# A two-layer metaformer on one core: pieces of a step's preparation at other units, the image read in front of the weights, column copies on VectorE alone, an image's first inputs through GpSimd's queue

## The chip, the cores and the metric

The kernel runs on one core of one Trainium2 chip. The metric is the device time of one execution in microseconds (us). The engines are TensorE (PE; its weight loads are listed as PEld), VectorE (DVE), ScalarE (ACT), GpSimd (POOL) and SyncE (SP), which here only issues DMAs. Each engine works through its own instructions in the order in which they were put in its queue, and waits on semaphores for the others.

## The reference, cut to what matters

Two images of 96 channels and 128 x 128 pixels, float32, pass two layers. Layer 0 normalizes over the channels, runs four Mamba scans (along rows and along columns, each forwards and backwards), fuses their outputs, adds them to x, and then applies a feed-forward block with values rounded to an 8-bit float. Layer 1 does the same with a 3 x 3 convolution in place of the scans. The change touches layer 0's normalization and scans alone, of which this is the core for one direction:

```
xz = x @ in_w.T                      # 96 -> 2 * 192
xc, z = split(xz)
xc = silu(conv4(xc) + conv_b)        # four taps along the sequence
xdbl = xc @ xproj_w.T                # -> dt_raw (6), B (16), C (16)
dt = softplus(dt_raw @ dt_w.T + dt_b)
for t:                               # 16384 positions, 192 channels, 16 states
    h = exp(dt_t * A) * h + dt_t * B_t * u_t
    y = sum over the states of h * C_t
y = (y + D * xc) * silu(z)
out = y @ outp_w.T                   # 192 -> 96
```

## The kernel before, in words

For each image there are three stages: `normalize` (layer 0's normalization), `mamba` (the scan stage), and `ffn_and_conv` (all the rest). The image lives in SBUF as `acc`, 96 channels by 16384 positions.

**Constants.** Ahead of the first image, SP reads 13 weight tensors, and ScalarE, VectorE and TensorE derive `amat`, `dmat`, `inx` and `gmat` from them. Only after these does `normalize` issue the eight reads of image 0.

**normalize.** 32 tiles of 512 positions each run through a generator `layernorm`: TensorE centers, ScalarE squares, TensorE takes the mean, ScalarE does log and exp, VectorE multiplies. `together` advances the generators in turn, one tile a turn behind the other. The result `xn` is written to DRAM row by row (`xnr`), then transposed by eight strided copies of 2048 positions, of which VectorE and ScalarE take one half each, and written column by column (`xnc`).

**mamba.** Directions are taken in two pairs (rows and columns together; first forwards, then backwards), and a pair is cut into 32 steps of 512 positions: 64 steps an image. The 2 x 192 channels of a pair fill three groups `g` of 128 partitions. A step holds 24 *units*: for each group, eight pairs of states. Unit k of the loop over `k` does, on each engine in this order:

- at even k, SP fetches rows of B for units k + 6 and k + 7 (`fetch`, line 336's `row_tile`), broadcast from DRAM to 128 partitions, and GpSimd multiplies the rows of B for units k + 2 and k + 3 with dt * u (`feed`, which calls `b_part`: lines 345 and 347; line 347 adds the state that enters the step);
- `issue(k, 0)`: the pieces that were put at place 0 of this unit;
- VectorE scans the first state (line 357), then does the product of the unit before with C (line 445), on GpSimd instead for units 2 and 10 of a step (`by_pool`, line 364); ScalarE copies the last column of that unit to `hst` (line 446); TensorE sums the products over the states into PSUM (`sums`, line 361); where a group begins, VectorE multiplies the finished sum with silu(z) (`gated`, line 368);
- ScalarE computes the decays exp(dt * A) of unit k + 2 (line 353, two activations);
- VectorE scans the second state;
- at even k, SP fetches rows of C for units k + 4 and k + 5;
- `issue(k, 1)`: the pieces that were put at place 1 of this unit.

Beside this runs the *prologue* of the next step, cut into pieces, and each piece has a unit and a place in a list written out by hand (`at`). With m counted from 24 units ahead of the step's own unit 0:

- `load`: SP reads the two inputs `xa` (from `xnr`) and `xb` (from `xnc`).
- `conv` for group 1, 0, 2: TensorE's in-projection with the four taps folded in, into the PSUM tile `misc`, of which there is one; `conv_out` (ScalarE) takes it from there. Group 1 holds channels of both directions, and goes through the tile `mix` and two DMAs (`mix`) to interleave them. `silu` (ScalarE) loads another function table, works on all three groups, and loads the first table back.
- `rows`, `rows_out`, `rows_to_dram`: dt_raw, B and C rows by TensorE, copied by ScalarE, written to DRAM by SP for the broadcast reads.
- for each group the *dt chain*: `dt_in` (TensorE), `dt_exp` and `dt_ln` (three ScalarE activations each), `dt_q`, `dt_log`, `dt_sum`, `dt_u` (one GpSimd operation each, lines 295, 298, 301, 305). Its temporaries `e`, `q`, `ln` have one buffer each.
- `gate`, `gate_out`: the z half of the in-projection; `silu` on it.
- `entry` (ScalarE, line 310) and `entering` (GpSimd, line 313): the state that enters the step.

After a group pair is finished, `project` (TensorE) and `collect` (ScalarE) add its output to `acc`.

All order is the program's own: inside these stages a manual schedule keeps each engine's instructions in the order in which the code issues them. Within one unit and place, pieces keep the order of the list, which puts the pieces that empty `misc` first.

The list stands in `prologue`, the loop at the end of `mamba`:

Of the kernel before, what the change touches and what calls it, by code (L numbers as in the profile page):

```python
# [10 lines left out]
F32 = mybir.dt.float32  # L11
# [30 lines left out]
def tile_metaformer(ctx: ExitStack, tc: tile.TileContext, a: dict, out: bass.AP):  # L42
# [19 lines left out]
    ident = const("ident", (128, 128))  # L62
    center = cpool.tile([C, C], F32, name="center")
# [14 lines left out]
    with tc.tile_pool(name="prep", bufs=1) as pp, tc.tile_pool(name="prep_ps", bufs=2, space=PSUM) as pps:  # L78
        alog = pp.tile([128, 2, NG, S], F32, name="alog")
        nc.sync.dma_start(alog, a["alog"])  # L80
        nc.scalar.activation(alog, alog, AF.Exp)
        nc.vector.tensor_scalar_mul(amat, alog, -1.0)

        dskip = pp.tile([128, 2, NG], F32, name="dskip")
        nc.sync.dma_start(dskip, a["dskip"])
        for pi in range(2):
            for g in range(NG):
                nc.vector.tensor_scalar_mul(dmat[:, pi, g, :], ident, dskip[:, pi, g : g + 1])

        inxw = pp.tile([C, 4, DI], F32, name="inxw")  # L90
        nc.sync.dma_start(inxw, a["inx"])
        taps = pp.tile([C, 4, 4, DI], F32, name="taps")
        nc.sync.dma_start(taps, a["taps"].broadcast_to((C, 4, 4, DI)))
        for d in range(4):
            nc.vector.tensor_tensor(inx[:, d], taps[:, d], inxw[:, d, None, :].broadcast_to((C, 4, DI)), ALU.mult)
        outx = pp.tile([C, 2, NG + 1, 128], F32, name="outx")
        nc.sync.dma_start(outx, a["outx"])
        fusew = pp.tile([C, 4, C], F32, name="fusew")
        nc.sync.dma_start(fusew, a["fusew"])
        for pi, pair in enumerate(PAIRS):  # L100

            for g in range(NG + 1):
                ps = pps.tile([128, C], F32, name="ps")
                nc.tensor.matmul(ps, outx[:, pi, g, :], fusew[:, pair[g // 2], :], start=True, stop=True)
                nc.vector.tensor_copy(gmat[:, pi, g, :], ps)
# [37 lines left out]
    blk = 4 * T  # L143

    def read(b, acc, j):

        nc.sync.dma_start(acc[:, bass.ts(j, blk)], a["x"][b, :, bass.ts(j, blk)])

    def normalize(b, acc, xnr, xnc):

        with ExitStack() as st:
            pool = lambda n, bufs, **kw: st.enter_context(tc.tile_pool(name=n, bufs=bufs, **kw))
            full, wp, psp = pool("n1", 1), pool("n2", 3), pool("n_ps", 3, space=PSUM)
            in_order(st)
            nc.scalar.preload_act_table_set("natural_log_exp_and_others")
            xn = full.tile([C, L], F32, name="xn")
            for j in range(L // blk if b == 0 else 1):
                read(b, acc, j if b == 0 else L // blk - 1)

            def one(r):  # L160
                sl = bass.ts(r, T)
                yield from layernorm(acc[:, sl], eps_c[0:C, 0:1], xn[:, sl], wp, psp, 5)
                if (r + 1) % 4 == 0:
                    sl = bass.ts(r // 4, blk)
                    nc.sync.dma_start(xnr[:, sl], xn[:, sl])

            together(*((r, one(r)) for r in range(NT)))
            cols = xn.rearrange("c (h w) -> c w h", w=W)
            for j in range(L // blk):
                stg = wp.tile([C, blk], F32, name="stg")  # L170
                half = blk // W // 2
                for i, eng in enumerate((nc.vector.tensor_copy, nc.scalar.copy)):
                    eng(
                        stg[:, i * half * W : (i + 1) * half * W].rearrange("c (w h) -> c w h", h=W),
                        cols[:, j * 2 * half + i * half : j * 2 * half + (i + 1) * half, :],
                    )
                nc.sync.dma_start(xnc[:, bass.ts(j, blk)], stg)

    def mamba(acc, xnr, xnc):

        with ExitStack() as st:
            pool = lambda n, bufs, **kw: st.enter_context(tc.tile_pool(name=n, bufs=bufs, **kw))
            io, one, two, gen = pool("io", 2), pool("one", 1), pool("two", 2), pool("gen", 4)
# [23 lines left out]
            def prologue(pi, i, d):  # L207
# [5 lines left out]
                def load():  # L213
                    for n, dram in (("xa", xnr), ("xb", xnc)):
                        t = io.tile([C, T + 3], F32, name=n)
                        if i == 0:
                            nc.gpsimd.memset(t[:, T : T + 3] if rev else t[:, 0:3], 0.0)
                            nc.sync.dma_start(t[:, 0:T] if rev else t[:, 3 : T + 3], dram[:, lo : lo + T])
                        else:
                            nc.sync.dma_start(t, dram[:, lo : lo + T + 3] if rev else dram[:, lo - 3 : lo + T])  # L220
# [20 lines left out]
                def mixed(name):  # L241
                    d["mix", name] = one.tile([128, T], F32, name="mix")
                    return d["mix", name]
# [74 lines left out]
                at = [(-2, 1, load), (2, 1, partial(mix, "xc")), (6, 1, partial(silu, "xc"))]  # L318
                at += [(13, 1, partial(mix, "sz")), (28 if first else 22, 1, partial(silu, "sz"))]
                at += [(9, 0, rows), (10, 0, rows_out), (10, 1, rows_to_dram)]  # L320
                for g, k in ((1, 1), (0, 3), (2, 5)):
                    at += [(k, 0, partial(conv, g)), (k + 1, 0, partial(conv_out, g))]
                for g, k in ((1, 12), (0, 17), (2, 20)):
                    at += [(k, 0, partial(gate, g)), (k + 1, 0, partial(gate_out, g))]
                dts = ((24, 25, 26, 27), (31, 32, 33, 34)) if first else ((14, 15, 16, 18), (19, 20, 21, 23))
                for g, ks in enumerate(((10, 11, 12, 14), *dts)):
                    at += [(k, 0, partial(f, g)) for k, f in zip(ks, (dt_in, dt_exp, dt_ln, dt_q))]
                    at += [(ks[3] + m, 0, partial(f, g)) for m, f in ((1, dt_log), (1, dt_sum), (2, dt_u))]
                    if i > 0:
                        at += [((17, 23, 27)[g], 0, partial(entry, g)), (20 + 8 * g, 1, partial(entering, g))]  # L330

                outs = (conv_out, gate_out, rows_out, dt_exp)
                return sorted(at, key=lambda p: (p[0], p[1], getattr(p[2], "func", p[2]) not in outs))
# [60 lines left out]
            def later(k, where, f, *args):  # L394
                todo.setdefault((k, where), []).append(partial(f, *args))

            def issue(k, where):
                for f in todo.pop((k, where), ()):
                    f()

            for k, where, f in prologue(*steps[0], state[0]):
                if k < nu:
                    f()
                else:
                    later(k - nu, where, f)

            def prepare(n):
                if n < len(steps):
                    for m, where, f in prologue(*steps[n], state[n]):
# [3 lines left out]
                        else:  # L413
                            later(k, where, f)
# [24 lines left out]
            def behind(k):  # L439
# [16 lines left out]
                if (g, s) in BY_POOL:  # L456
                    later(k + 1, 1, by_pool, h, c)
                    later(k + 3, 1, sums, s, y, c)
# [4 lines left out]
                if s == S - 2 and g > 0:  # L463
                    later(k + 3, 0, project, pi, i, d, g)
                    later(k + 3, 1, collect, pi, d, g)
# [7 lines left out]
            for k in range(total + 6):  # L473
                n, u = divmod(k, nu)
                if u == nu - 2:
# [120 lines left out]
    acc = accp.tile([C, L], F32, name="acc")  # L596
# [77 lines left out]
```

## Time and profile before

| | |
|---|---|
| median of 3 runs | 12153.81 us (12136.48 to 12159.19) |
| the profiled execution's own time | 12198.56 us |
| its span | 12196.8 us |
| VectorE busy | 10962.5 us, 90% |
| TensorE busy | 10601.0 us, 87% |
| GpSimd busy | 9908.7 us, 81% |
| ScalarE busy | 8585.5 us, 70% |
| first scan of image 0, of image 1 | at 151.4 us, at 6234.8 us |
| last scan of image 0, of image 1 | ends at 5532.9 us, at 11618.2 us |
| last layernorm product of image 0, of image 1 | ends at 81.1 us, at 6166.7 us |
| bytes moved by DMA | 3417 MB, 280 GB/s in the mean |

How to read the lines that follow: a line of a timeline gives the start in us from the start of the span, the duration in us, the engine, the line of the kernel, the operation, the tile written and the tiles read, the shapes, the count, and in brackets the idle time of the engine just before and what ended it. A group's line gives count, busy time, mean duration in ns, and the idle time before its instructions. Idle time of an engine counts only where that engine, or one that waits for it, is the one that sets the end.

### The profile page before, as it was taken

The page shows a single profiled execution, that of the slowest core. Times are in us where ns is not written, and L with a number is a line of the kernel's source. Part 1 is how long each engine was busy: PE and PEld are TensorE (multiplying, and loading weights), DVE is VectorE, ACT ScalarE, POOL GpSimd, SP SyncE. Part 2 cuts the span into 40 slices and gives each one's busy share as a digit, 9 for nine tenths or more (in the row PEclk, how much of TensorE's full clock was granted, in tenths as well). Part 3 has the DMA queues.
Part 4 walks back from the last instruction along what each step waited for, and adds up shares of the span by engine and source line. Part 5 has one row for each costly group of instructions (what it writes and reads, how often), then busy time and mean ns, then how long its engine had stood idle before and what let it go on. Part 6 is the DMA issues. An engine that isn't in the chain of part 4 may idle for free. (4 is left out here: it accounts for less than half of the span.)

```text
span 12196.8 us, 95712 instructions
## 1 busy us (share of the span) xinstructions
PE 10601.0 (87%) x24208; PEld 4012.8 (33%) x24208; DVE 10962.5 (90%) x10624; ACT 8585.5 (70%) x15110; POOL 9908.7 (81%) x5336
## 2 busy tenths in 40 slices
PE   7888888888888888888978888888888888888889
PEld 2333333333333333333323333333333333333333
DVE  6999999999999999995469999999999999999954
ACT  6777777777777777775577777777777777777655
POOL 5998999999998989891159989999989999988811
PEclk9999999999999999999989999999999999999999
DMA  7887888788877878781068888888878878878700
GB/s 250 309 319 302 307 319 313 309 318 312 318 310 306 319 305 310 308 317 47 26 242 307 308 317 312 314 318 313 313 307 308 321 308 316 314 305 309 304 32 13
DMA packets 539169, 3417.07 MB, mean 280 GB/s; under 512 B 67276, under 2 KB 68396, under 8 KB 140696
## 3 DMA queue, kind: packets, MB, share of 16 engines
q1 hardware_dynamic: 538616, 3410.94, 72.9%
q8 instruction: 195, 3.19, 0.1%
q14 instruction: 358, 2.93, 0.1%
HBM read 3289.04 MB, written 54.53 MB: 274 GB/s over the span
## 5 line engine op out<-in xcount | busy, mean ns | idle before, releaser
L345 POOL TENSOR_TENSOR row<-dtu,row 128x2048 f32<-128x2048 f32 x1536 | 6949.9, 4525 | 820.8 <-DMA row<-bcd 658.5
L357 DVE TENSOR_TENSOR_SCAN da<-da,row 128x512 f32<-128x512 f32 x5632 | 6650.2, 1215 | 509.8 <-ACT da L353 187.3
L361 PE MATMUL y<-row,ident 128*128 128x512 f32 x12288 | 5957.9, 618 | 1130.5 <-DVE row L445 1125.7
L353 ACT ACTIVATE da<-dt,amat 128x512 f32<-128x512 f32 x6144 | 4250.4, 692 | 278.7 <-DVE row L357 92.0
L361 PEld LDWEIGHTS y<-row,ident 128*128 128x128 f32 x12288 | 2268.5, 194 | 4643.0 <-issue 2296.4
L445 DVE TENSOR_TENSOR row<-da,row 128x1024 f32<-128x1024 f32 x2816 | 3395.8, 1206 | 1.0 <-DMA row<-bcd 0.9
L446 ACT COPY hst<-da 128x2 f32<-128x2 f32 x2816 | 434.7, 154 | 1423.8 <-DVE row L445 1412.4
L204 PE MATMUL misc<-xa,inx 96*64 96x512 f32 (+1 forms) x2048 | 963.6, 614 | 131.3 <-DMA xa<-xnr 108.0
L204 PE MATMUL misc<-xb,inx 96*64 96x512 f32 (+1 forms) x2048 | 962.3, 613 | 1.9 <-ACT xc L231 1.6
L568 POOL TENSOR_TENSOR acc<-acc,y 96x512 f32<-96x512 f32 x128 | 147.4, 1152 | 987.1 <-DVE y L567 987.1
L357 DVE TENSOR_TENSOR_SCAN row<-da,row 128x512 f32<-128x512 f32 x512 | 616.9, 1205 | 0.0
L364 POOL TENSOR_TENSOR row<-row,row 128x1024 f32<-128x1024 f32 x256 | 602.8, 2355 | 7.1 <-DVE row L357 6.1
L580 PE MATMUL pc<-pad,kw 96*96 96x512 f32 x1152 | 566.7, 593 | 0.0
L452 PE MATMUL y<-xc,dmat 128*128 128x512 f32 x768 | 428.9, 640 | 145.2 <-DVE sz L368 145.2
L295 POOL TENSOR_TENSOR q<-e,q 128x512 f32<-128x512 f32 x384 | 487.5, 1270 | 71.5 <-ACT q L292 71.5
L204 PEld LDWEIGHTS misc<-xa,inx 96*64 96x64 f32 (+1 forms) x2048 | 329.7, 166 | 650.6 <-issue 444.9
L231 ACT ACTIVATE xc<-misc,convb 128x512 f32<-128x512 f32 x256 | 175.8, 687 | 519.7 <-PE misc L204 519.7
L301 POOL TENSOR_TENSOR dt<-dt,ln 128x512 f32<-128x512 f32 x384 | 487.1, 1269 | 30.1
L298 POOL TENSOR_TENSOR ln<-ln,q 128x512 f32<-128x512 f32 x384 | 487.2, 1269 | 20.1
L305 POOL TENSOR_TENSOR dtu<-dt,xc 128x512 f32<-128x512 f32 x384 | 487.1, 1269 | 10.2
L378 PE MATMUL misc<-sz,gmat 128*96 128x512 f32 x1024 | 483.6, 594 | 0.0
L124 DVE TENSOR_TENSOR xq<-xm,rs 96x512 fp8e5<-96x512 f32 x128 | 87.9, 687 | 388.0 <-ACT rs L120 387.9
(81 smaller groups left out, 9340.4 us busy)
## 6 DMA issues: line engine op xcount, KB each, us to landing
row<-bcd SPq DMA_DIRECT2D x3072, 1024.0 KB, 7.1
xc<-mix SPq DMA_DIRECT2D x256, 128.0 KB, 5.3
sz<-mix SPq DMA_DIRECT2D x256, 128.0 KB, 5.4
xa<-xnr SPq DMA_DIRECT2D x124, 193.1 KB, 5.2
xb<-xnc SPq DMA_DIRECT2D x124, 193.1 KB, 5.5
bcd<-rows SPq DMA_DIRECT2D x128, 128.0 KB, 6.7
acc<-in_x_dram SPq DMA_DIRECT2D x16, 768.0 KB, 8.6
xnr<-xn SPq DMA_DIRECT2D x16, 768.0 KB, 4.3
```

Of the source, the lines that this page charges most:

```text
L204: nc.tensor.matmul(ps[rows, :], w(PAIRS[pi][d], k, lo, hi), src[d][:, k : k + T], **se)
L295: nc.gpsimd.tensor_tensor(d["q"], d["e"], d["q"], ALU.subtract)
L298: nc.gpsimd.tensor_tensor(d["ln"], d["ln"], d["q"], ALU.add)
L301: nc.gpsimd.tensor_tensor(d["dt"][g], d["dt"][g], d["ln"], ALU.add)
L305: nc.gpsimd.tensor_tensor(dtu, d["dt"][g], d["xc"][:, g, :], ALU.mult)
L345: nc.gpsimd.tensor_tensor(b, d["dtu"][g][:, None, :].broadcast_to((128, 4, T)), b, ALU.mult)
L353: nc.scalar.activation(da[:, j, :], d["dt"][g], AF.Exp, scale=amat[:, pi, g, s + j : s + j + 1])
L357: nc.vector.tensor_tensor_scan(h[:, j, :], da[:, j, :], b[:, j, :], 0.0, ALU.mult, ALU.add)
L361: nc.tensor.matmul(y, ident, c[:, j, :], start=False, stop=s + j == S - 1)
L364: nc.gpsimd.tensor_tensor(c, h, c, ALU.mult)
L445: nc.vector.tensor_tensor(c, h, c, ALU.mult)
L580: nc.tensor.matmul(pc, kw[:, t, :], rows, start=t == 0, stop=t == 8)
```

## The change

**The prologue's pieces stand at other units.** `load` moves from -2 to -3; conv of groups 1, 0, 2 from units 1, 3, 5 to 1, 5, 9, and `conv_out` from place 0 to place 1 of the unit after; `silu` of xc from 6 to 11; `rows` from 9 to 13 and its two followers with it; `gate` from 12, 17, 20 to 11, 18, 21; the dt chains of the three groups, which began at 10, 14 and 19, begin at 15, 17 and 22, and their `dt_q` stands at place 1 of units 17, 22 and 26; `silu` of sz from 22 (28 in the first step) to 31, that is unit 7 of the step itself; `entry` and `entering` move a few units back; `project` and `collect` one unit later. Pieces of different steps that meet at one unit and place are now ordered together, those that empty `misc` first; `rank` carries that.

**The image is read in front of the weights.** `acc` and the reads of image 0 stand right after `ident`; what derives weights becomes a generator `prep` that runs among the layernorm tiles from turn 8 on, and its own reads are issued there.

**Column copies.** 16 copies of 1024 positions, all on VectorE, from a pool of three buffers that is opened after the layernorm tiles.

**First inputs.** For an image's first step in the forward pair, `xa` and `xb` are read through GpSimd's queue. Pools of `mamba` are opened in another order, and `mix` has a pool of its own.

```diff
     ident = const("ident", (128, 128))
+    acc = accp.tile([C, L], F32, name="acc")
+    blk = 4 * T
+
+    def read(b, acc, j):
+
+        nc.sync.dma_start(acc[:, bass.ts(j, blk)], a["x"][b, :, bass.ts(j, blk)])
+
+    for j in range(L // blk):
+        read(0, acc, j)
...
+        alog, dskip = load("alog", (128, 2, NG, S)), load("dskip", (128, 2, NG))
+        outx, fusew = load("outx", (C, 2, NG + 1, 128)), load("fusew", (C, 4, C))
+        inxw, taps = load("inx", (C, 4, DI)), load("taps", (C, 4, 4, DI), spread=True)
+        yield
...
-            full, wp, psp = pool("n1", 1), pool("n2", 3), pool("n_ps", 3, space=PSUM)
+            wp, psp = pool("n2", 3), pool("n_ps", 2, space=PSUM)
...
-            together(*((r, one(r)) for r in range(NT)))
+            streams = [(r, one(r)) for r in range(NT)]
+            with ExitStack() as weights:
+                together(*streams, *([(8, prep(weights))] if b == 0 else []))
+            stg = pool("n3", 3)
             cols = xn.rearrange("c (h w) -> c w h", w=W)
-            for j in range(L // blk):
-                stg = wp.tile([C, blk], F32, name="stg")
-                half = blk // W // 2
-                for i, eng in enumerate((nc.vector.tensor_copy, nc.scalar.copy)):
...
+            part = 8
+            for j in range(W // part):
+                t = stg.tile([C, part, W], F32, name="stg")
+                nc.vector.tensor_copy(t, cols[:, bass.ts(j, part), :])
+                nc.sync.dma_start(xnc[:, bass.ts(j, part * W)], t.rearrange("c w h -> c (w h)"))
...
-            io, one, two, gen = pool("io", 2), pool("one", 1), pool("two", 2), pool("gen", 4)
+
+            io, gen, one, mixp, two = (pool(*p) for p in (("io", 2), ("gen", 4), ("one", 1), ("mixp", 1), ("two", 2)))
...
-                            nc.sync.dma_start(t[:, 0:T] if rev else t[:, 3 : T + 3], dram[:, lo : lo + T])
+                            queue = nc.sync if rev else nc.gpsimd
+                            queue.dma_start(t[:, 0:T] if rev else t[:, 3 : T + 3], dram[:, lo : lo + T])
...
-                at = [(-2, 1, load), (2, 1, partial(mix, "xc")), (6, 1, partial(silu, "xc"))]
-                at += [(13, 1, partial(mix, "sz")), (28 if first else 22, 1, partial(silu, "sz"))]
-                at += [(9, 0, rows), (10, 0, rows_out), (10, 1, rows_to_dram)]
-                for g, k in ((1, 1), (0, 3), (2, 5)):
-                    at += [(k, 0, partial(conv, g)), (k + 1, 0, partial(conv_out, g))]
-                for g, k in ((1, 12), (0, 17), (2, 20)):
-                    at += [(k, 0, partial(gate, g)), (k + 1, 0, partial(gate_out, g))]
-                dts = ((24, 25, 26, 27), (31, 32, 33, 34)) if first else ((14, 15, 16, 18), (19, 20, 21, 23))
-                for g, ks in enumerate(((10, 11, 12, 14), *dts)):
-                    at += [(k, 0, partial(f, g)) for k, f in zip(ks, (dt_in, dt_exp, dt_ln, dt_q))]
+                at = [(-3, 1, load), (3, 0, partial(mix, "xc")), (11, 1, partial(silu, "xc"))]
+                at += [(13, 0, partial(mix, "sz")), (31, 1, partial(silu, "sz"))]
+                at += [(13, 0, rows), (14, 1, rows_out), (15, 0, rows_to_dram)]
+                for g, k in ((1, 1), (0, 5), (2, 9)):
+                    at += [(k, 0, partial(conv, g)), (k + 1, 1, partial(conv_out, g))]
+                for g, k, out in ((1, 11, (12, 1)), (0, 18, (19, 0)), (2, 21, (22, 0))):
+                    at += [(k, 0, partial(gate, g)), (*out, partial(gate_out, g))]
+                dts = ((24, 25, 26, 27), (31, 32, 33, 34)) if first else ((17, 18, 20, 22), (22, 23, 24, 26))
+                for g, ks in enumerate(((15, 16, 17, 17), *dts)):
+                    at += [(k, 0, partial(f, g)) for k, f in zip(ks, (dt_in, dt_exp, dt_ln))]
+                    at += [(ks[3], 1, partial(dt_q, g))]
                     at += [(ks[3] + m, 0, partial(f, g)) for m, f in ((1, dt_log), (1, dt_sum), (2, dt_u))]
                     if i > 0:
-                        at += [((17, 23, 27)[g], 0, partial(entry, g)), (20 + 8 * g, 1, partial(entering, g))]
+                        at += [((20, 25, 29)[g], 0, partial(entry, g)), ((21, 28, 36)[g], 1, partial(entering, g))]
...
-                    later(k + 1, 1, by_pool, h, c)
-                    later(k + 3, 1, sums, s, y, c)
+                    later(k + 1, 1, True, by_pool, h, c)
+                    later(k + 3, 1, True, sums, s, y, c)
...
-                    later(k + 3, 0, project, pi, i, d, g)
-                    later(k + 3, 1, collect, pi, d, g)
+                    later(k + 4, 0, True, project, pi, i, d, g)
+                    later(k + 5, 1, False, collect, pi, d, g)
...
-                if u == nu - 2:
+                if u == nu - 3:
```

## The prediction

> **What bounds the kernel now.** I read the busy times by stage first, then the groups of instructions, then one undisturbed step of the scan stage engine by engine in order of time. I call a scan pair a unit (24 to a step, unit 0 to 23, g = u // 8), and give places in a unit in us from its first scan.
>
> Busy time by stage, the second stage being the scan stage of image 0:
>
> ```profile
> core 0: us, PE busy (x) PEld busy (x) DVE busy (x) ACT busy (x) POOL busy (x), PEclk, DMA share, GB/s
> ...
> 151.40:5532.90 5381.50, 4688.50 (x10557) 1770.15 (x10554) 5177.93 (x4670) 3888.08 (x6879) 4869.73 (x2591) 0.98 0.81 311
> ```
>
> Both scan stages take 5381.5 and 5383.4 us, 88% of the span; VectorE is busy 96% of them and GpSimd 90%. A step costs 5381.5 / 64 = 84.09 us. Groups, scans and GpSimd's products:
>
> ```profile
> L345 POOL TENSOR_TENSOR row<-dtu,row 128x2048 f32<-128x2048 f32 x1536 | 6949.9, 4525 | 820.8 <-DMA row<-bcd 658.5
> L357 DVE TENSOR_TENSOR_SCAN da<-da,row 128x512 f32<-128x512 f32 x5632 | 6650.2, 1215 | 509.8 <-ACT da L353 187.3
> ```
>
> VectorE's timeline in the step that begins at 1834.33:
>
> ```profile
> 1847.88 1.23 DVE L357 TENSOR_TENSOR_SCAN da<-da,row 128x512 f32<-128x512 f32 x1 [0.39 <-POOL row L347]
> ...
> 1855.96 1.23 DVE L357 TENSOR_TENSOR_SCAN da<-da,row 128x512 f32<-128x512 f32 x1 [1.23 <-ACT hst L446]
> 1857.10 1.21 DVE L445 TENSOR_TENSOR row<-da,row 128x1024 f32<-128x1024 f32 x1
> ...
> 1860.47 1.20 DVE L445 TENSOR_TENSOR row<-da,row 128x1024 f32<-128x1024 f32 x1
> ...
> 1866.76 1.23 DVE L357 TENSOR_TENSOR_SCAN da<-da,row 128x512 f32<-128x512 f32 x1 [0.59 <-ACT da L353]
> ```
>
> A free unit lasts 3.365 us (1857.10 to 1860.47); units 1, 9 and 17 carry line 368 and last 3.96; units 3 and 11, whose product GpSimd does, 2.4. Without stalls a step is 19 x 3.365 + 3 x 3.96 + 2 x 2.4 = 80.6 us. So 3.5 us of the mean step are stalls. In this one (83.1 us) they stand at units 4, 6 and 9: ScalarE is behind TensorE's conv at 6 and 9, GpSimd late at 4. The rest of the mean comes from disturbed steps, where TensorE waited for xa or ran at half clock. GpSimd's part of the same step:
>
> ```profile
> 1870.07 4.52 POOL L345 TENSOR_TENSOR row<-dtu,row 128x2048 f32<-128x2048 f32 x1 [4.90 <-DMA row<-bcd]
> 1874.67 0.20 POOL L347 TENSOR_TENSOR row<-row,enter 128x4 f32<-128x4 f32 x1
> 1874.82 2.35 POOL L364 TENSOR_TENSOR row<-row,row 128x1024 f32<-128x1024 f32 x1
> 1877.14 4.52 POOL L345 TENSOR_TENSOR row<-dtu,row 128x2048 f32<-128x2048 f32 x1
> ...
> 1881.88 0.22 POOL L313 TENSOR_TENSOR enter<-enter,hst 128x16 f32<-128x16 f32 x1
> ...
> 1886.81 1.27 POOL L295 TENSOR_TENSOR q<-e,q 128x512 f32<-128x512 f32 x1
> 1888.15 1.27 POOL L298 TENSOR_TENSOR ln<-ln,q 128x512 f32<-128x512 f32 x1
> 1889.50 1.27 POOL L301 TENSOR_TENSOR dt<-dt,ln 128x512 f32<-128x512 f32 x1
> 1890.73 4.53 POOL L345 TENSOR_TENSOR row<-dtu,row 128x2048 f32<-128x2048 f32 x1
> ```
>
> Start to start, a feed (L345 + L347) takes 4.75, a dt operation 1.35 (1.24 ahead of a feed), by_pool 2.33, entering 0.18. A step holds 12 feeds, 12 dt operations, 2 by_pool, 3 entering: 57 + 15.5 + 4.7 + 0.5 = 77.7 us, against 80.6 us of unstalled VectorE. Its only gaps in this step are the 4.90 us shown and 0.51 at 1860.36. It is the second bound, 3 us behind the first.
>
> [...] no feed passes the dt operation ahead of it. [...] after only 1.85 us idle in unit 12, the four matmuls of unit 13 took 1.06 us each, not 0.59. [...] The loads take 1.28 us here, but a silu with both loads occupies ScalarE for 4.08 us in all[...]. [...]
>
> **The change part by part.** *Conv at units 1, 5, 9 instead of 1, 3, 5, outs after the decays.* Eight matmul slots of 0.43 us, 3.44 us each, are as many as before; they no longer pile up, and ScalarE no longer waits ahead of a decay. ScalarE has 3.365 - 1.55 (hst and two decays) = 1.8 us free in a unit, and each unit's pieces now fit or have a unit to recover. The 1.23 and 0.59 go, and with them most of what disturbed steps add: about 3 of the 3.5 us. What is late next is GpSimd.
>
> *The dt chain later.* dt_q(0) moves from unit 14 to the end of 17, dt_q(1) from 18 to 22, dt_q(2) from 23 to unit 2 of the next step, each with two more operations behind it. In GpSimd's instruction order dt_q(0) is a barrier: it waits for ScalarE's dt_ln(0), and the feeds stand behind it. From it to the feed of the next step's units 6 and 7 stand 6 feeds, 11 dt operations, one by_pool, one entering: 28.5 + 14.4 + 2.33 + 0.18 = 45.4 us with nothing to wait for.
>
> How early can dt_q(0) start? hst(15) follows unit 16's product (2.35), two decays end its slot at 3.9, that is 0.54 in unit 17; then dt_ln(0), in the trace of before 2.09 us from its first activation to its last result (1891.32 to 1893.41). So 2.65 in unit 17. From there VectorE reaches the next unit 6 in 1.31 + 6 x 3.365 + 3.365 + 3.96 + 3.365 + 2.4 + 2 x 3.365 = 41.3 us. GpSimd lacks 4.1 us: VectorE must stall that long, at unit 6. From unit 6 to 17 GpSimd has only 32.4 us to do in 39 and idles at the barrier; the lead can't be carried past it. Floor of a step: 36.6 (units 6 to 16) + 2.65 + 45.4 = 84.65 us, already above 84.09.
>
> *TensorE ahead of it.* ScalarE does conv_out(2) at 0.53 of unit 11, hst and decays, silu(xc) (4.08), hst and decays, then gate_out(1), which ends at 3.1 of unit 13. The single misc bank makes rows wait for that. Then TensorE does rows (2.58), three units' sums (12, the deferred 10, 13; 1.72 each) and dt_in(0) (0.86): its result comes at 1.8 of unit 16, where ScalarE could have taken it at 0.54. dt_exp(0) (1.66), hst and decays (1.55) and dt_ln(0) follow: dt_q(0) starts at 3.8 of unit 17. Step: 36.6 + 3.8 + 45.4 = 85.8 us. TensorE was idle some 2.5 us twice just before (units 12 and 13), so rows may run at half clock, which costs up to 4 x 0.43 = 1.7: 87.5 us. I take that for one step in three: 86.4. That is +2.3 on 84.09; with 63 such steps an image, 126 x 2.3 = +290 us.
>
> *Loads one unit earlier, DMAs.* xa, xb are issued 3.4 us sooner on SP's queue; in disturbed steps of before TensorE waited up to 2.7 us for them, which ends there; it is in the size of before's mean. rows_to_dram goes from unit 10 to 15 and holds SP's next row loads till rows_out, but these land units ahead of GpSimd, which is late itself: nothing, unless GpSimd were early, then up to the 4.90 us seen above. The c rows of unit 16 wait for the deferred sums and may stop VectorE up to 1.9 us in unit 17; the barrier hangs on ScalarE, not on that, so it is part of the same stall. silu(sz) at unit 7 ends 2 us before line 368 wants it in unit 9: nothing.
>
> *The start of an image.* In image 1 the copies begin at 6166.70 and the first conv at 6192.98, after all of them. With the inputs on GpSimd's queue and buffers clear of the copies, conv needs the first piece alone: 1 (copy) + 5 (landing) + 5.5 (xb as on SP[...]) = about 12 instead of 26 us, less 2 because mix stands behind 16 writes on SP. So -12 each (0 to -20). Copies on VectorE alone cost nothing: the writes (17.7 us) pace them. Image 0: the first xm starts at 20.8; with x ahead of the weights some 12 us sooner, but the weights now wait on SP behind the first xnr write, and their VectorE steps stand in front of layernorm's: -8 (+5 to -14). Together -32. The tail's collect one unit later: under 1 us.
>
> **Sum.** 290 - 32 = +258 us. Against the profiled execution, 12198.6 + 258 = 12457; the median of the runs is 45 us below it, so 12153.8 + 258 = 12412: 12410.
>
> **Rivals.** *Floor*: TensorE delivers in time and clock, 84.65: 126 x 0.56 - 32 = +39, 12193; against it stands the one misc bank. *Heavier*: half clock at every step and a little disturbance, 87.9: +480 - 20, about 12615; for it the idle gaps of 2.5 us. *The other side*: GpSimd isn't held by the barrier, so the stalls simply go: steps of 81.0, 126 x -3.1 - 32 = -423, 11731. For it: GpSimd's total of 77.7 fits in 80.6. It needs dt_q(0) 4.1 us before its earliest place, or shorter feeds; any gain decides at 84.35 us a step, 0.3 us below the floor. The 4.52 us of a feed doesn't vary in the trace, and nothing passes in that queue. *The change does not what it says*: the changed program's GpSimd order has dt_q(0) ahead of these feeds, so only the start of the images can fail, +32.
>
> **How the numbers follow.** Main case (12300 to 12550) 0.64, floor case 0.15 (a fifth of it within 0.2%), heavier 0.13, other side 0.08. Left out of 12230 to 12580: the other side, half the floor, a third of the heavier. About 0.2% is what a measurement tells from no change: faster 0.08, same 0.03, slower 0.89.
>
> **What would show it.** Right: VectorE idle before the scans of unit 6, released by GpSimd's product, 4 to 7 us a step; no stall released by ScalarE at 4, 5, 9; GpSimd idle before dt_q(0) until ScalarE's q. Wrong: steps under 84.3 us, or those stalls released by ScalarE or a DMA.

## The result, and the profile after

| | before | after |
|---|---|---|
| median of 4 runs | 12148.27 us (12136.48 to 12159.19) | 12514.99 us (12508.62 to 12520.89) |
| the profiled execution's own time | 12198.56 us | 12508.62 us |
| scan stage of image 0, of image 1 | 5381.5, 5383.4 us | 5553.7, 5551.3 us |
| mean step | 84.1 us | 86.8 us |

The changed kernel is slower: ratio 1.0302, 95% interval 1.0284 to 1.032. Line numbers below are those of the changed kernel: scan L368, product with C L456, feed L356 and L358, `by_pool` L375, `dt_q` L304, `dt_log` L307, `dt_sum` L310, `dt_u` L314, `entering` L322, `dt_in` L285, rows L267, sums L372, `gated` L379, `hst` L457, decay L364. Busy time by stage after the change, the second stage being the scan stage of image 0, from its first scan to the end of its last:

```profile
core 0: us, PE busy (x) PEld busy (x) DVE busy (x) ACT busy (x) POOL busy (x), PEclk, DMA share, GB/s
0.00:136.40 136.40, 92.04 (x196) 32.55 (x198) 45.17 (x72) 75.11 (x123) 13.57 (x14) 0.82 0.68 202
136.40:5690.10 5553.70, 4696.96 (x10563) 1746.62 (x10560) 5173.07 (x4670) 3873.04 (x6879) 4872.91 (x2591) 0.98 0.79 302
5690.10:6378.80 688.70, 610.51 (x1537) 232.60 (x1537) 308.12 (x639) 389.53 (x667) 86.82 (x78) 0.94 0.16 47
```

No engine has more to do: VectorE is busy 5173 us in the stage (5178 before) and GpSimd 4873 (4870). The stage is 172 us longer all the same, so the time is idle time. The groups of the page say at which instructions:

```profile
L368 DVE TENSOR_TENSOR_SCAN da<-da,row 128x512 f32<-128x512 f32 x5632 | 6626.3, 1214 | 656.9 <-POOL row L358 578.7
L356 POOL TENSOR_TENSOR row<-dtu,row 128x2048 f32<-128x2048 f32 x1536 | 6950.2, 4525 | 12.6 <-DMA row<-bcd 9.3
...
L456 DVE TENSOR_TENSOR row<-da,row 128x1024 f32<-128x1024 f32 x2816 | 3398.5, 1207 | 161.8 <-DMA row<-bcd 161.5
...
L304 POOL TENSOR_TENSOR q<-e,q 128x512 f32<-128x512 f32 x384 | 487.5, 1269 | 961.7 <-ACT hst L457 885.3
```

The idle time of the scans is now ended for the most part by GpSimd's feed (578.7 us), where before ScalarE's decays led with 187.3. GpSimd's own idle time has moved: in front of its feeds stood 820.8 us, most of it ended by DMAs; now 12.6 us stand there, and 961.7 in front of `dt_q`. Split by unit, over both images, the stalls of VectorE are 496 us at unit 6 and 90 at unit 22, both ended by GpSimd's feed, and 161 at unit 17 (the rows of C). Those released by ScalarE, at units 5, 6 and 9 before, are gone.

Most steps are of one of two kinds, 86.1 and 87.8 us, the first a little more frequent. GpSimd from the barrier of a step of the first kind to the feed of the next unit 6; its unit 17 began at 2016.81:

```profile
2020.86 1.27 POOL L304 TENSOR_TENSOR q<-e,q 128x512 f32<-128x512 f32 x1 [6.26 <-ACT hst L457]
2022.08 4.53 POOL L356 TENSOR_TENSOR row<-dtu,row 128x2048 f32<-128x2048 f32 x1
...
2054.98 0.20 POOL L358 TENSOR_TENSOR row<-row,enter 128x4 f32<-128x4 f32 x1
2055.14 1.27 POOL L304 TENSOR_TENSOR q<-e,q 128x512 f32<-128x512 f32 x1
2056.48 1.27 POOL L307 TENSOR_TENSOR ln<-ln,q 128x512 f32<-128x512 f32 x1
2057.83 1.27 POOL L310 TENSOR_TENSOR dt<-dt,ln 128x512 f32<-128x512 f32 x1
2059.06 2.36 POOL L375 TENSOR_TENSOR row<-row,row 128x1024 f32<-128x1024 f32 x1
2061.37 4.53 POOL L356 TENSOR_TENSOR row<-dtu,row 128x2048 f32<-128x2048 f32 x1
2065.98 0.21 POOL L358 TENSOR_TENSOR row<-row,enter 128x4 f32<-128x4 f32 x1
```

No later line of this stretch carries a bracket: GpSimd idles 6.26 us at the barrier and then works 45.3 us without a gap that the trace lists (2020.86 to 2066.19). What `dt_q(0)` reads is finished by ScalarE's `dt_ln(0)` 0.08 us earlier (2020.78); the bracket names the small copy that ScalarE did right behind that:

```profile
2018.75 0.61 ACT L298 ACTIVATE q<-e 128x512 f32<-128x512 f32 x1
2019.40 0.63 ACT L300 ACTIVATE ln<-q 128x512 f32<-128x512 f32 x1
2020.06 0.72 ACT L301 ACTIVATE q<-q,minus_one 128x512 f32<-128x512 f32 x1
2020.69 0.14 ACT L457 COPY hst<-da 128x2 f32<-128x2 f32 x1
```

The three dt operations at 2055.14 are chain 2, which the change put ahead of the feed of units 6 and 7. VectorE at the other end of it:

```profile
2061.04 1.22 DVE L368 TENSOR_TENSOR_SCAN da<-da,row 128x512 f32<-128x512 f32 x1
2066.22 1.23 DVE L368 TENSOR_TENSOR_SCAN da<-da,row 128x512 f32<-128x512 f32 x1 [3.96 <-POOL row L358]
```

The scan starts 0.03 us after the feed ends. Leaving out the first and the last step of each image, that is so in all of the 124 steps that remain.

What divides the two kinds of step is the rows on TensorE. A step of the second kind, then one of the first:

```profile
1914.60 1.98 PE L372 MATMUL y<-row,ident 128*128 128x512 f32 x4 [2.34 <-DVE row L456]
1918.73 4.51 PE L267 MATMUL misc<-xc,bcw 128*96 128x512 f32 x6 [2.14 <-ACT hst L457]
...
2002.36 1.99 PE L372 MATMUL y<-row,ident 128*128 128x512 f32 x4 [2.35 <-DVE row L456]
2006.48 2.81 PE L267 MATMUL misc<-xc,bcw 128*96 128x512 f32 x6 [2.14 <-ACT hst L457]
```

The same six matmuls after the same two gaps take 4.51 and 2.81 us. The granted clock of TensorE over these two stretches is 0.62 and 1.00 of full speed; in the slow one it is 0.50 from 1919.64 to 1923.05. Counted over all steps, they take more than 3.3 us in 61 of 128, with a granted clock of 0.50 to 0.73 over them, and in the other 67 it is 1.00. In the slow one `dt_q(0)` starts at 5.75 of unit 17, in the other at 4.05. With the formula of the prediction: 36.6 + 4.05 + 45.4 = 86.05 and 36.6 + 5.75 + 45.4 = 87.75, where 86.1 and 87.8 are measured.

### The profile page after: what moved, and what is told of

The parts are those of the page before. It is cut to its first block, busy times and chain, and to the rows that moved or that the text cites. A ratio compares the mean times of both kernels' runs of the same rounds, so it can differ in the third digit from the quotient of the medians.

```text
span 12506.9 us, 95887 instructions
## 1 busy us (share of the span) xinstructions
PE 10619.9 (85%) x24208; PEld 3961.1 (32%) x24208; DVE 10969.2 (88%) x10640; ACT 8528.1 (68%) x15094; POOL 9920.9 (79%) x5340
## 5 line engine op out<-in xcount | busy, mean ns | idle before, releaser
L368 DVE TENSOR_TENSOR_SCAN da<-da,row 128x512 f32<-128x512 f32 x5632 | 6626.3, 1214 | 656.9 <-POOL row L358 578.7
L356 POOL TENSOR_TENSOR row<-dtu,row 128x2048 f32<-128x2048 f32 x1536 | 6950.2, 4525 | 12.6 <-DMA row<-bcd 9.3
L372 PE MATMUL y<-row,ident 128*128 128x512 f32 x12288 | 5828.6, 608 | 1185.1 <-DVE row L456 1184.1
L364 ACT ACTIVATE da<-dt,amat 128x512 f32<-128x512 f32 x6144 | 4248.9, 692 | 194.1 <-DVE row L368 1.7
L372 PEld LDWEIGHTS y<-row,ident 128*128 128x128 f32 x12288 | 2272.6, 192 | 4580.1 <-issue 2306.3
L456 DVE TENSOR_TENSOR row<-da,row 128x1024 f32<-128x1024 f32 x2816 | 3398.5, 1207 | 161.8 <-DMA row<-bcd 161.5
L457 ACT COPY hst<-da 128x2 f32<-128x2 f32 x2816 | 438.3, 156 | 2448.0 <-DVE row L456 2442.5
L304 POOL TENSOR_TENSOR q<-e,q 128x512 f32<-128x512 f32 x384 | 487.5, 1269 | 961.7 <-ACT hst L457 885.3
L212 PE MATMUL misc<-xa,inx 96*64 96x512 f32 (+1 forms) x2048 | 954.4, 608 | 85.2 <-ACT acc L395 58.3
L375 POOL TENSOR_TENSOR row<-row,row 128x1024 f32<-128x1024 f32 x256 | 603.3, 2357 | 256.8 <-issue 246.7
L267 PE MATMUL misc<-xc,bcw 128*96 128x512 f32 x768 | 457.8, 743 | 234.0 <-ACT hst L457 221.0
L290 ACT ACTIVATE e<-misc,dtb 128x512 f32<-128x512 f32 x384 | 261.6, 681 | 561.8 <-PE misc L285 291.6
L368 DVE TENSOR_TENSOR_SCAN row<-da,row 128x512 f32<-128x512 f32 x512 | 617.3, 1206 | 0.2
L310 POOL TENSOR_TENSOR dt<-dt,ln 128x512 f32<-128x512 f32 x384 | 487.7, 1270 | 30.1
L307 POOL TENSOR_TENSOR ln<-ln,q 128x512 f32<-128x512 f32 x384 | 487.6, 1270 | 20.1
L314 POOL TENSOR_TENSOR dtu<-dt,xc 128x512 f32<-128x512 f32 x384 | 488.8, 1273 | 10.2
## 6 DMA issues: line engine op xcount, KB each, us to landing
xa<-xnr SPq DMA_DIRECT2D x124, 193.1 KB, 8.0
xb<-xnc SPq DMA_DIRECT2D x124, 193.1 KB, 8.4
```

Source lines behind the costliest of these rows:

```text
L212: nc.tensor.matmul(ps[rows, :], w(PAIRS[pi][d], k, lo, hi), src[d][:, k : k + T], **se)
L304: nc.gpsimd.tensor_tensor(d["q"], d["e"], d["q"], ALU.subtract)
L307: nc.gpsimd.tensor_tensor(d["ln"], d["ln"], d["q"], ALU.add)
L310: nc.gpsimd.tensor_tensor(d["dt"][g], d["dt"][g], d["ln"], ALU.add)
L314: nc.gpsimd.tensor_tensor(dtu, d["dt"][g], d["xc"][:, g, :], ALU.mult)
L356: nc.gpsimd.tensor_tensor(b, d["dtu"][g][:, None, :].broadcast_to((128, 4, T)), b, ALU.mult)
```

## The experiments

The theory: the order of GpSimd's queue makes `dt_q(0)` a barrier, and the step lasts as long as VectorE's units 6 to 16, the place Q of `dt_q(0)` in unit 17, and GpSimd's uninterrupted 45.4 us. The rivals name the lateness of the rows of C, or ScalarE, or half clock as the cause by itself, or hold that GpSimd's amount of work is what counts, wherever it stands. In the runs of each experiment the kernel before took 12150 to 12158 us.

**The starts of the images alone.** The units of the list, and the orders that go with them, are those of before; the early read of x, the column copies and the first inputs through GpSimd's queue are kept.

```diff
-                at = [(-3, 1, load), (3, 0, partial(mix, "xc")), (11, 1, partial(silu, "xc"))]
+                at = [(-2, 1, load), (2, 1, partial(mix, "xc")), (6, 1, partial(silu, "xc"))]
...
-                dts = ((24, 25, 26, 27), (31, 32, 33, 34)) if first else ((17, 18, 20, 22), (22, 23, 24, 26))
-                for g, ks in enumerate(((15, 16, 17, 17), *dts)):
+                dts = ((24, 25, 26, 27), (31, 32, 33, 34)) if first else ((14, 15, 16, 18), (19, 20, 21, 23))
+                for g, ks in enumerate(((10, 11, 12, 14), *dts)):
```

> The changed kernel with the old units for every piece of the prologue: only the start of the images, the column copies, the first inputs' queue and the pools are changed. If the units alone make the kernel slower (mine): steps of 84.1 us as before, first scans 15 and 13 us sooner, so about 30 us below before, 12118. If the new pools, copies or the queue carry part of the loss: above 12148, up to 12515.

Measured: 12122.77 us (12109.06 to 12142.58), ratio 0.9971 (0.996 to 0.9982): -35 us. So the starts give a little, and the loss is in the moved pieces.

**The deferred sums one unit sooner.** TensorE's sums of unit 10 no longer stand between the rows and `dt_in(0)`.

```diff
-                    later(k + 3, 1, True, sums, s, y, c)
+                    later(k + 2 + (g == 0), 1, True, sums, s, y, c)
```

> The changed kernel with the deferred sums of unit 10 issued one unit sooner, ahead of rows. Mine, that the start of dt_q(0) sets the step: TensorE's idle gap ahead of rows is filled, dt_in(0) comes 1.2 to 1.7 us sooner, dt_q(0) starts near 2.7 in unit 17 in all steps, 84.7 to 84.9 us a step instead of 86.8, about 12270. If the wait for the C rows at unit 17 is a cost of its own: only its 1.2 us a step go and GpSimd's stall at unit 6 stays at 4.0, about 12365. If only the half clock matters: the 87.8 us steps become 86.1, about 12415.

Measured: 12310.62 us (12308.09 to 12313.86), ratio 1.0127 (1.011 to 1.0144). Nearly all steps last 85.3 us, and the stall at unit 17 is gone, while the one at unit 6 is as large as before. The rows run at full clock, but the sums put ahead of them don't:

```profile
1883.96 5.38 PE L372 MATMUL y<-row,ident 128*128 128x512 f32 x8 [2.34 <-DVE row L456]
1889.18 2.74 PE L267 MATMUL misc<-xc,bcw 128*96 128x512 f32 x6
```

Eight sums take 5.38 us at a granted clock of 0.68, where eight behind `dt_in(0)` take 3.70 in the changed kernel. `dt_q(0)` starts at 3.35 of unit 17, and 36.6 + 3.35 + 45.4 = 85.35. The mechanism holds. My size was half a microsecond a step too low, since I had let half clock vanish with the order. A stall on the rows of C can go without the stall at unit 6 going. But the new place of the sums brings the rows of C and `dt_q(0)` sooner by nearly as much, so this run alone doesn't tell their costs apart.

**One GpSimd operation of each chain left out.** `dt_log` (line 307), and with it the term ln + q of dt, is left out for all three groups: three operations of 1.35 us less between barrier and feed.

```diff
-                    nc.gpsimd.tensor_tensor(d["ln"], d["ln"], d["q"], ALU.add)
+                    pass
```

> The changed kernel without line 307 (dt_log, the addition of the correction to the logarithm is left out; three GpSimd operations of 1.35 us a step). Mine: three of them lie between dt_q(0) and the feed of units 6 and 7, so the 3.96 us stall at unit 6 all but goes, 82.8 us a step, about 12010. If ScalarE's or TensorE's lateness sets the step: no change, 12500.

Measured: 11919.61 us (11914.48 to 11920.39), ratio 0.9803 (0.9789 to 0.9818). The page of this run:

```profile
L368 DVE TENSOR_TENSOR_SCAN da<-da,row 128x512 f32<-128x512 f32 x5632 | 6610.6, 1213 | 131.2 <-POOL row L358 63.7
```

The wait for the feed falls from 578.7 to 63.7 us. The mean step is 82.1 us; the formula gives 36.6 + 4.05 + 41.35 = 82.0 with rows at full clock, and 82.4 with the 33 slow ones of 128 that this run has. The time is 90 us below my figure. Of the 595 us (12515 - 11920), the stretch from barrier to feed gives the most: it shrinks from 45.3 to 41.0 us, and 126 x 4.3 = 542. Another 48 go with half clock: the rows are slow in 33 steps, not 61, and 28 x 1.7 = 48. So GpSimd's work behind the barrier is paid in full. Why fewer rows are slow is taken up below, with the clock.

**The same operation left out of the kernel before** (the same term of dt missing, line 298 there).

```diff
-                    nc.gpsimd.tensor_tensor(d["ln"], d["ln"], d["q"], ALU.add)
+                    pass
```

> The kernel before without dt_log (the same addition is left out). Mine: GpSimd is late only at unit 4 there, 0.4 us a step, and the stalls released by ScalarE stay: 50 to 100 us less, 12080. If GpSimd's total sets the step in both kernels: as much as in the changed one, 600 us less, 11560.

Measured: 12146.36 us (12127.58 to 12187.55), ratio 0.9997 (0.9987 to 1.0007).

```profile
L357 DVE TENSOR_TENSOR_SCAN da<-da,row 128x512 f32<-128x512 f32 x5632 | 6638.6, 1214 | 475.0 <-ACT da L353 191.0
```

Four microseconds less work a step on GpSimd change nothing there, not even the 50 to 100 us that I expected. VectorE's waits for GpSimd at unit 4 go (49.8 us, now 0.2), but ScalarE's decays still end as much idle time (187.3, now 191.0), and its copies to `hst` more (157.8, now 171.0). GpSimd's 77.7 us a step were never the bound before. The order made them one, which speaks against the rival that only the amount counts.

**The rows sooner.** Rows at unit 12, ahead of `gate(1)`, chain 0 one unit sooner, to make the barrier early.

```diff
-                at += [(13, 0, partial(mix, "sz")), (31, 1, partial(silu, "sz"))]
-                at += [(13, 0, rows), (14, 1, rows_out), (15, 0, rows_to_dram)]
+                at += [(17, 0, partial(mix, "sz")), (31, 1, partial(silu, "sz"))]
+                at += [(12, 0, rows), (13, 1, rows_out), (14, 0, rows_to_dram)]
...
-                for g, k, out in ((1, 11, (12, 1)), (0, 18, (19, 0)), (2, 21, (22, 0))):
+                for g, k, out in ((1, 15, (16, 1)), (0, 18, (19, 0)), (2, 21, (22, 0))):
...
-                for g, ks in enumerate(((15, 16, 17, 17), *dts)):
+                for g, ks in enumerate(((14, 15, 16, 16), *dts)):
```

> The changed kernel with rows one unit sooner, gate(1) behind dt_exp(0) instead of ahead of rows, and the chain of group 0 one unit sooner (14, 15, 16, 16). Work and GpSimd's order behind dt_q(0) are the same, but dt_q(0) no longer waits for gate_out(1). Mine: dt_q(0) starts about 3.7 us sooner, near 3.7 of unit 16, and the step shrinks by as much: 82.3 to 84 us a step, 11950 to 12170. If what counts is how many GpSimd operations stand between units and not when the first can start: no change, 12500.

Measured: 12312.96 us (12308.87 to 12314.57), ratio 1.0127 (1.0112 to 1.0142). A miss by 140 us or more. Steps are 85.3 us. TensorE, then VectorE around unit 17 (which begins at 1902.04) of a step of this run:

```profile
1886.94 5.43 PE L267 MATMUL misc<-xc,bcw 128*96 128x512 f32 x6 [4.04 <-ACT xc L260]
1892.17 5.47 PE L372 MATMUL y<-row,ident 128*128 128x512 f32 x12
1897.57 1.12 PE L285 MATMUL misc<-rows,dtw 12*128 12x512 f32 x2
```

```profile
1902.04 1.23 DVE L368 TENSOR_TENSOR_SCAN da<-da,row 128x512 f32<-128x512 f32 x1 [1.25 <-ACT da L364]
1903.18 1.21 DVE L456 TENSOR_TENSOR row<-da,row 128x1024 f32<-128x1024 f32 x1
1905.29 0.69 DVE L379 TENSOR_TENSOR sz<-y,sz 128x512 f32<-128x512 f32 x1 [0.90 <-PE y L372]
```

TensorE now stands 4.04 us waiting for silu(xc), runs all the rows at half clock (5.43 us, 1.06 us each, granted clock 0.50), and has twelve sums before `dt_in(0)`, which begins in unit 16 as late as in the run with the sums sooner (0.23 of it in both). ScalarE waits there with a decay queued behind `dt_exp(0)`, so VectorE stalls 1.25 us, and 0.90 us more for TensorE's sums. `dt_q(0)` starts at 2.01 of unit 17, but that unit itself comes 1.3 us later: 40.0 us after unit 6, as against 36.6 + 3.35 = 39.95 with the sums sooner. Add 45.4: 85.4. What I had overlooked is that moving the rows ahead of the gate doesn't move silu(xc), for which the rows wait and behind which `gate_out(1)` had stood in ScalarE's queue. The formula holds, but this run says nothing for or against an earlier barrier, since it didn't make one. It does show how stalls add up: here 262 us stand at unit 17 and 285 at unit 6, with the sums sooner none and 493, and with the barrier 40.0 us behind unit 6 in both, both have the same step. What VectorE waits earlier in the step it doesn't wait at unit 6.

**Chain 2 behind the feeds.** `dt_q(2)` with its three followers goes from unit 26 to 31, and `entry` of that group with them from 29 to 34, so three dt operations (4.05 us) stand behind the feed of units 6 and 7, and work and barrier stay as they are.

```diff
-                dts = ((24, 25, 26, 27), (31, 32, 33, 34)) if first else ((17, 18, 20, 22), (22, 23, 24, 26))
+                dts = ((24, 25, 26, 27), (31, 32, 33, 34)) if first else ((17, 18, 20, 22), (22, 23, 24, 31))
...
-                        at += [((20, 25, 29)[g], 0, partial(entry, g)), ((21, 28, 36)[g], 1, partial(entering, g))]
+                        at += [((20, 25, 34)[g], 0, partial(entry, g)), ((21, 28, 36)[g], 1, partial(entering, g))]
```

> The changed kernel with dt_q(2) and the three operations behind it five units later (31 instead of 26) and entry(2) at 34: the same work, but three operations of 1.35 us no longer stand between dt_q(0) and the feed of units 6 and 7. Mine: 45.4 becomes 41.35 us, steps of 82.0 and 83.7 us, about 12000. If the stall only moves on to units 8 to 14: 12400 and more. If it isn't GpSimd's order: 12510.

Measured: 11969.21 us (11965.32 to 11985.33), ratio 0.9852 (0.9838 to 0.9867).

```profile
L368 DVE TENSOR_TENSOR_SCAN da<-da,row 128x512 f32<-128x512 f32 x5632 | 6637.7, 1214 | 168.0 <-POOL row L358 89.3
...
L456 DVE TENSOR_TENSOR row<-da,row 128x1024 f32<-128x1024 f32 x2816 | 3393.7, 1205 | 100.5 <-DMA row<-bcd 100.2
```

Steps of 82.1 and 83.8, for which the formula gives 36.6 + 4.05 + 41.35 = 82.0 and 36.6 + 5.75 + 41.35 = 83.7. The stall at unit 6 is gone (0.3 us in all). The bound is still the same: VectorE has waited at units 17 (97 us) and 22 (90 us, for GpSimd), and then comes to unit 6 just as the feed ends, with the scan 0.03 us behind it in 121 of 124 steps. No work was removed. One chain's position in GpSimd's queue is worth 546 us (12515 - 11969): the stretch from barrier to feed shrinks from 45.3 to 41.4 us, some 495 us, and rows slow in 34 steps, not 61, give some 46. Of all the runs this one bears most on the cause.

**A feed ahead of the barrier.** The sums sooner, and `dt_q(0)` from unit 17 to 18, behind the feed of units 20 and 21. In this run group 0's `dt_q` reads the `e` of group 1, because `dt_exp(1)` is issued first and puts its own tile in the place of `d["e"]`; group 0's dt is changed by that.

```diff
-                for g, ks in enumerate(((15, 16, 17, 17), *dts)):
+                for g, ks in enumerate(((15, 16, 17, 18), *dts)):
```

> d_sums_sooner with dt_q(0) one unit LATER (18 instead of 17), so that the feed of units 20 and 21 passes ahead of it. Mine: dt_q(0) starts 0.9 us later, but 4.75 us of feed leave the chain behind it: 85.3 becomes 81.5 us a step, about 11830. If the lateness of the dt chain itself is what costs, and not the feeds behind the barrier: 86.2 us or more, 12420.

Measured: 12129.73 us (13 runs, 12116.64 to 12141.38), ratio 0.998 (0.9972 to 0.9989). A miss by 300 us. The barrier doesn't start behind the feed, but waits again:

```profile
2122.76 4.54 POOL L356 TENSOR_TENSOR row<-dtu,row 128x2048 f32<-128x2048 f32 x1 [2.00 <-DMA row<-bcd]
2127.38 0.20 POOL L358 TENSOR_TENSOR row<-row,enter 128x4 f32<-128x4 f32 x1
2129.24 1.27 POOL L304 TENSOR_TENSOR q<-e,q 128x512 f32<-128x512 f32 x1 [1.66 <-ACT e L293]
```

The wait is for the last activation of `dt_exp(1)`, which ScalarE works off in unit 18: I had moved the reader past the piece that writes `e` next. In this step `dt_q(0)` starts at 2.31 of unit 18: 36.6 + 3.96 (unit 17) + 2.31 + 40.65 (45.4 without the feed that passed) = 83.5, and most steps are 83.1 to 83.8.

**The same, with its own `e`.** `dt_q(0)` at place 0 of unit 18, ahead of `dt_exp(1)`.

```diff
-                    at += [(ks[3], 1, partial(dt_q, g))]
+                    at += [(ks[3], int(g > 0), partial(dt_q, g))]
...
-                outs = (conv_out, gate_out, rows_out, dt_exp)
+                outs = (conv_out, gate_out, rows_out, dt_exp, dt_q)
```

> The run e_feed_first again, but with dt_q(0) ahead of dt_exp(1) in unit 18 (place 0), so that it reads its own group's e and doesn't wait for ScalarE's dt_exp(1). In e_feed_first GpSimd was free 0.16 us into unit 18 and waited 2.20 for that e. Mine: dt_q(0) starts 0.2 us into unit 18, behind the feed; step = 36.6 (units 6 to 16) + 3.96 (unit 17) + 0.2 + 40.65 (the 45.4 of GpSimd's work without that feed) = 81.4 us against 83.6, and 126 x 2.2 = 280 below e_feed_first's 12130: 11850 us, with a stall of about 0.8 at unit 6. Rival: dt_exp(1) now waits on ScalarE for dt_q(0), and three group-1 activations and the decays of unit 20 behind it come 1.4 us later, so ScalarE takes the place of GpSimd as it does in the kernel before: decays late by 1 to 2 us a step at units 20 to 22, 83 us a step, 12030 us or more.

Measured: 11898.09 us (11894.33 to 11903.74), ratio 0.9791 (0.9767 to 0.9816). GpSimd, and ScalarE:

```profile
1829.88 4.53 POOL L356 TENSOR_TENSOR row<-dtu,row 128x2048 f32<-128x2048 f32 x1 [2.31 <-DVE da L368]
1834.49 0.20 POOL L358 TENSOR_TENSOR row<-row,enter 128x4 f32<-128x4 f32 x1
1834.64 1.27 POOL L304 TENSOR_TENSOR q<-e,q 128x512 f32<-128x512 f32 x1
```

```profile
1835.94 0.69 ACT L290 ACTIVATE e<-misc,dtb 128x512 f32<-128x512 f32 x1 [1.35 <-POOL q L304]
```

The barrier has no wait left: ScalarE is early and GpSimd comes straight from the feed. It starts at 0.88 of unit 18 in this step, 0.72 in the mean, rather than 0.2, since the feed itself waits for a scan to free its row tile; 36.6 + 3.96 + 0.72 + 40.65 = 81.9, and 82.0 is the mean measured. That is why the time lies 48 us above my figure. ScalarE does wait 1.35 us for `dt_q(0)`, as the rival said, but VectorE's scans wait for ScalarE's decays only 0.4 us in both images together.

**Both: a feed ahead of the barrier, chain 2 behind the feeds.** First on the run with the changed `e`, then on the one with its own.

> Both: e_feed_first with group 2's chain at 31. Mine: no stall at unit 6 is left, GpSimd's 77.7 us fit in the step of 80.6, about 80.8 us a step, 11740. If another wait takes over (rows from DRAM, ScalarE): as e_feed_first or above, 11830.

Measured: 11723.03 us (11721.3 to 11724.48), ratio 0.9647 (0.9633 to 0.9661).

> The same, with group 2's chain (dt_q at 31, entering at place 1 of unit 36 as it was but its ScalarE copy at 34) behind the feeds as in g_both, all chains reading their own e. Mine: GpSimd is no longer what VectorE waits for, a step costs VectorE's own 80.6 us to 80.8: 11725 us, as g_both's 11723, and 3.5% below the kernel before. Rival: the wait of dt_exp(1) for dt_q(0) on ScalarE costs 1 to 2 us a step at units 20 to 22, which chain 2's place doesn't change: 11850 to 11980 us.

Measured: 11729.24 us (11725.66 to 11730.33), ratio 0.965 (0.9631 to 0.967). The page of this last one:

```profile
L368 DVE TENSOR_TENSOR_SCAN da<-da,row 128x512 f32<-128x512 f32 x5632 | 6596.8, 1213 | 74.7 <-POOL row L356 64.7
```

Nearly every step lasts 80.6 us, VectorE's own time, and no unit has a regular stall; 60 of the 64.7 us stand before the first scans of the two images. This version beats both kernels: 3.5% below before, about 6.3% below the changed kernel (11729.24 / 12514.99). Its moves of pieces, the ones that took ScalarE's stalls away, are those of the change; different are the places of chains 0 and 2 on GpSimd, of one unit's sums on TensorE, and of `entry` of group 2 on ScalarE.

## Why the prediction was right, and what it mis-sized

*The barrier and the formula: right.* The last run has the same instructions as the changed kernel and takes 786 us less (12514.99 - 11729.24); only places in the queues differ. Chain 2's place alone is worth 546 us. In the changed kernel and all runs with its units whose steps are bound this way, the formula gives the step within 0.3 us. The bound itself can be seen: in the two last runs, which it no longer holds, not one scan of unit 6 starts within 0.1 us of the end of its feed. It is a sum because GpSimd takes its work in the order of its queue: in the trace of after it idles 126 times ahead of a `dt_q` till ScalarE is done, 885.3 us in all, with the feeds left behind it, and in the 45.3 us shown above nothing is exchanged and no gap is listed. (The "two more operations" behind each `dt_q` are three; the 11 dt operations of the sum count them so.)

*Conv apart, ScalarE no longer ahead of decays: right.* No stall at units 5 and 9 is left, and once GpSimd's and TensorE's order are mended, 80.6 us a step come out: the 3.5 us of stalls that the prediction read from before are all to be had. The gain was there, and the new order of GpSimd's queue took back more than that.

*TensorE's lateness, Q = 3.8: 0.25 too low.* Rows began at 3.1 of unit 13 as worked out. But rows, sums and `dt_in` came to 2.05 of unit 16 rather than 1.8. Q was 4.05.

*Half clock in one step of three: mis-sized.* It cost the 1.7 us expected, but came in 61 of 128 steps; the share was a guess. With the term before it the mean step is 86.8 and not 86.4: 340 us for both scan stages where the sum had 290. (Of the four matmuls that the prediction read in the trace of before, three took 1.06 us and the first 0.74. The granted clock there is 0.50 from 1879.39 to 1882.80; the first began at 1878.87, ahead of that.) In the changed kernel the same gaps of 2.34 and 2.14 us, with matmuls between, stood ahead of half clock in one step and of full clock in the next. The trace of after holds 220 stretches of granted clock, 1.00 and 0.50 in turn, and all of them begin on one grid of 3.413 us, to within 0.01 us. Take the time at which the rows start by this grid: over 1.125 us of it 66 of 68 steps are fast, over the rest of it 58 of 59 are slow. So in this execution the share of slow steps goes with how the length of the step runs against the grid. That this also made the slow rows fewer in the run with chain 2 behind the feeds and in the one without `dt_log` (34 and 33 of 128) is my estimate, from their steps of about 82 us. The steps of 85.3 us in two of the runs are 25 times 3.413, so that each would meet the clock where the last one did; whether the clock holds them at that length, no run tells.

*The starts of the images, -32: right in the sum.* The first scan comes 15.0 us sooner in image 0 (151.4, now 136.4), where 20 were forecast. From the last scan of image 0 to the first of image 1 it is 688.7 us where it was 701.9, 13.2 less for 12, and the tail is 1.9 shorter: -30. The run with the starts alone gives -35. The first inputs on GpSimd's queue took 5.7 us (`xa`) and 4.0 (`xb`) from issue to landing, so the 5.5 for `xb`, taken as on SP, was too high.

*From the profiled execution to the median: the largest miss.* The prediction took off 45 us for both kernels. That belonged to one execution of before, 50 us above the median; after's profiled execution lies 6 us below its own. This term is 51 of the 105 us by which the time was missed. The steps are 50, the starts 2, and the rest rounding. The run with the starts alone, profiled in an execution at its median, suggests where the 45 us came from: it has the units of before, and scan stages of 5344.7 and 5366.2 us instead of 5381.5 and 5383.4. So 84.09 was probably no typical mean of before; about 83.7 was.

*The rows of C at unit 17: right in place.* 161 us stand there, and 90 at unit 22, which the prediction didn't name. Neither adds to the step: what VectorE waits there it needn't wait at unit 6, as the sums sooner and the rows sooner show side by side.

*Still open:* what brings half clock. The same gaps of 2.34 and 2.14 us on TensorE were followed by a granted clock of 0.62 in one step and 1.00 in the next.

## What to carry to other kernels

Where an engine keeps the order of its queue, as GpSimd did here, an instruction that waits for another engine is a barrier for all behind it (885.3 us of idle time in the changed kernel): add up what stands between it and the next instruction that the bottleneck waits for, without a gap, and compare that with the bottleneck's own time over the same stretch. GpSimd, with 77.7 us of work a step, made the step 86.8 us where VectorE needs 80.6, because the idle time ahead of its barrier (6.26 us in the step shown) couldn't be used behind it; the cure that needs no less work is to put a due piece of work ahead of the barrier, and what nobody waits for yet behind the due work. When a reader is moved in such a queue, look for the next writer of what it reads.

## What the runs showed of the hardware that wasn't expected

- Gaps of 2.34 and 2.14 us on TensorE, 1.98 us of matmuls between them, were followed by six matmuls in 4.51 us in one step and 2.81 in another. Eight sums after one gap of 2.34 us took 5.38 us. After 4.04 us idle the six took 5.43. In the trace of after, granted clocks of 1.00 and 0.50 change on a grid of 3.413 us that runs through the whole execution, and where on it the rows start tells the slow steps from the fast in 124 of 127.
- The reads of `xa` take 8.0 us from issue to landing in the median where they took 5.2 before, with the same 193.1 KB each. The other unit of the loads can't be all of it: in the four runs with the sums sooner they stand at this unit too and take 5.2 to 5.3. The idle time in front of the matmuls on `xa` fell all the same, from 131.3 to 85.2 us.
- A ScalarE wait of 1.35 us in unit 18, with decays queued behind it, stopped VectorE's scans for no more than 0.4 us in 128 steps.
